# Edge counts beside the keys, x + b0 ahead of the degrees, and one more step inside layer 0's norm

## Chip, cores and metric

The kernel runs on one core of one Trainium2 chip, in one launch. The metric is the device time of that launch in microseconds; it was 4014.03 us before the change (median of 3 runs, 4009.7 to 4014.95).

## What is computed

Two graph layers over 32 batches of 512 nodes with 128 features; the adjacency has about one edge in sixteen and its diagonal. Cut to what matters:

```
# layer 0
a = adj + I;  degree = a.sum(2);  d = degree ** -0.5  (0 where infinite)
x = layernorm(x + d * (a @ (d * (x @ weight))) + bias)
# layer 1, for every pair of nodes i, j
pre = (x @ W1[:D])[j] + (x @ W1[D:])[i] + b1
msg = gelu(layernorm(pre) * g1 + be1)
agg[i] = sum over j of msg[i, j] * adj[i, j]
x = layernorm(x + layernorm(concat(x, agg) @ W2 + b2) * g2 + be2)
```

## The kernel before

**The sparse pairs.** Layer 1 does not form all pairs. For each node it picks the neighbours that exist, in 8 slots for each quarter of the nodes, one slot for the diagonal and two shared slots. The main loop runs over 32 batches, and in each over 41 *groups* (`order`: 8 slots of 4 groups, 1, and 2 of 4). Below, group k of a batch is the k-th of these 41, counted from 0. A group is a chain over four engines: TensorE builds `u` (16 bf16 matmuls, L724 and L725), VectorE adds and brings it to SBUF (`u_sb`, L734), ScalarE takes the gelu (`m`, four instructions at L763), GpSimd multiplies the selection with the adjacency (`sw`, L749), and TensorE adds it up (`agg`, L772). The chain is spread over the loop: iteration k issues u of group k, then `pass_on` issues agg of group k-3, u_sb and sw of group k-1 and m of group k-2. Three PSUM buffers hold u, so u of group k waits for u_sb of group k-3.

**The preparation.** While batch b runs its groups, batch b+1 is prepared by Python generators whose steps end at `yield`. `prepare(g)`, at the end of each iteration, advances them in the order of the list `plan`: layer0, lists, parts, factors, more, shared. A phase with n steps over w groups has done `n * (j + 1) // w` of them after its j-th group, so its step k (from 0) falls in group ceil(w(k+1)/n) - 1. `layer0` of batch b+1 has 26 steps over the groups 0 to 21 of batch b. `advance(todo)`, just before `prepare`, moves the generator `finish` of the batch that ended last.

**Steps of layer0, as far as they matter here.** Steps 1 to 4 transpose the adjacency on TensorE (`pa`, L249); one step later ScalarE sums rows (`copied`, L260) and copies the transpose (`a_t`, L261). Step 5 does this for the last quarter and lets VectorE make `mask` from the whole of `a_t` (L263). Step 6 is empty. Step 7 has the degrees on GpSimd (L277 to L287) and `xb` = x + b0 (L289), then on ScalarE four `counted` (L293, each sums one quarter of the mask into `edges`), `s` (L297) and `own_s` (L302). Steps 9 and 10 issue the two halves of `pconv` on TensorE (L311). Step 11 has `y` and its statistics on VectorE (L318, L194, L196); the norm's GpSimd part (L199 to L205) is step 12, its ScalarE part `x1` (L208) step 13; `x1` is transposed on TensorE (`pt_x1`, L220) in step 15. From step 21 on, each step makes a quarter of `key` on VectorE from a matmul `pv` (L361 to L365).

**Other work of the same groups.** `finish` of the batch before uses the same `layernorm` twice: `un` and, as the last, `o_sb`, with VectorE statistics, a GpSimd part and a ScalarE part, all at the same line numbers as layer 0's. `more` (L455 to L458) keeps VectorE at searching neighbours beyond the eighth, `shared` (L466 to L598) follows; in it ScalarE copies `sent` (L533) behind TensorE's `pl` (L537). The `edges` are read much later, in `shared` (L499).

**What sets the order.** Inside `manual_schedule` VectorE, ScalarE and GpSimd execute in the order of the program text. TensorE and the DMA queue of SyncE are ordered by the framework's scheduler. Every engine executes its own queue in order, and an instruction whose input is late holds back all behind it. Single-buffered tiles by tag (`t1`, `t2`, `t3`, `mask`, `copied`, `xs`) add waits for the last reader.

Of the kernel before, what the change touches and what calls it, by code (L numbers as in the profile page):

```python
# [8 lines left out]
F32 = mybir.dt.float32  # L9
BF16 = mybir.dt.bfloat16  # L10
I32 = mybir.dt.int32
U32 = mybir.dt.uint32
AF = mybir.ActivationFunctionType
ALU = mybir.AluOpType
# [4 lines left out]
P = 128  # L19
# [8 lines left out]
def bcast(ap, n):  # L28

    return ap.unsqueeze(1).to_broadcast([ap.shape[0], n, ap.shape[-1]])  # L30
# [16 lines left out]
def sparse_path(ctx, tc, x, adj, w0, b0, w1, b1, g1, be1, w2, b2, g2, be2, out, most):  # L47
# [21 lines left out]
    nc = tc.nc  # L69
    B, N, D = x.shape  # L70
    C = N // P
# [3 lines left out]
    node = ctx.enter_context(tc.tile_pool(name="node", bufs=1))  # L75
    small = ctx.enter_context(tc.tile_pool(name="small", bufs=2))
# [66 lines left out]
    rows = {}  # L143
# [41 lines left out]
    def rsqrt(dst, src):  # L185

        nc.gpsimd.tensor_tensor(dst, src, power[:, 0:1].to_broadcast([P, src.shape[-1]]), ALU.pow)  # L187

    def layernorm(src, dst, key):

        stats = small.tile([P, C, 6], F32, tag="stats", name=f"stats_{key}")
        mv = small.tile([P, C, 2], F32, tag="mv", name=f"mv_{key}")
        for c in range(C):
            nc.vector.bn_stats(stats[:, c, :], src[:, c, :])  # L194
        for c in range(C):
            nc.vector.bn_aggr(mv[:, c, :], stats[:, c, :])  # L196
        yield
        ve = small.tile([P, C], F32, tag="ve", name=f"ve_{key}")
        nc.gpsimd.tensor_scalar(ve, mv[:, :, 1], EPS, None, ALU.add)  # L199
        rstd = small.tile([P, C], F32, tag="rstd", name=f"rstd_{key}")  # L200
        rsqrt(rstd, ve)

        shift = small.tile([P, C], F32, tag="shift", name=f"shift_{key}")
        nc.gpsimd.tensor_tensor(shift, mv[:, :, 0], rstd, ALU.mult)  # L204
        nc.gpsimd.tensor_scalar(shift, shift, -1.0, None, ALU.mult)  # L205
        yield
        for c in range(C):
            nc.scalar.activation(  # L208
                dst[:, c, :], src[:, c, :], AF.Identity, bias=shift[:, c : c + 1], scale=rstd[:, c : c + 1]
            )  # L210
        yield

    def bank(key):
        return ps.tile([P, 512], F32, tag="ps", name=key)
# [6 lines left out]
        return pt  # L221

    state = {}

    def pause(n):

        for _ in range(n):
            yield

    def layer0(b):  # L230

        st = state[b] = {}
        xs = node.tile([P, C, D], F32, tag="xs", name=f"xs_{b}")
# [7 lines left out]
        edges = small.tile([P, C], F32, tag="edges", name=f"edges_{b}")  # L241
        st["edges"] = edges
        deg = small.tile([P, C], F32, tag="deg", name=f"deg_{b}")
        mask = big.tile([P, C, N], BF16, tag="mask", name=f"mask_{b}")
        px = transposed(xs, f"x_{b}")
        for mc in range(C):
# [12 lines left out]
            copied = small.tile([P, N], BF16, tag="copied", name=f"copied_{b}_{mc}", bufs=1)  # L259
# [11 lines left out]
            if mc == 0:  # L271
                x_t = node.tile([P, N], F32, tag="t0", name=f"x_t_{b}")
                nc.scalar.copy(x_t, px)
        yield from pause(2)

        deg1 = small.tile([P, C], F32, tag="deg1", name=f"deg1_{b}")
        nc.gpsimd.tensor_scalar(deg1, deg, 1.0, None, ALU.add)  # L277
# [7 lines left out]
        nc.gpsimd.tensor_sub(dinv, rdeg, none)  # L285
        dinv2 = small.tile([P, C], F32, tag="dinv2", name=f"dinv2_{b}", bufs=1)
        nc.gpsimd.tensor_tensor(dinv2, dinv, dinv, ALU.mult)  # L287
        xb = node.tile([P, C, D], F32, tag="t2", name=f"xb_{b}")
        nc.gpsimd.tensor_tensor(xb, xs, bcast(rows["b0"], C), ALU.add)  # L289

        for q in range(C):
            copied = small.tile([P, N], BF16, tag="copied", name=f"counted_{b}_{q}", bufs=1)
            nc.scalar.activation(copied, mask[:, q, :], AF.Copy, accum_out=edges[:, q : q + 1])  # L293

        s = node.tile([P, C, D], F32, tag="t1", name=f"s_{b}")
        for c in range(C):
# [4 lines left out]
        for c in range(C):  # L301
            nc.scalar.activation(  # L302
                own_s[:, c, :], psup[:, c * P : (c + 1) * P], AF.Copy, scale=dinv2[:, c : c + 1]
            )
        yield from pause(2)
        nc.gpsimd.tensor_tensor(xb, xb, own_s, ALU.add)
        pt = bank(f"pconv_{b}")
# [8 lines left out]
        y = node.tile([P, C, D], F32, tag="t3", name=f"y_{b}")  # L316
        for c in range(C):
            nc.vector.scalar_tensor_tensor(  # L318
                y[:, c, :], pt[:, c * P : (c + 1) * P], dinv[:, c : c + 1], xb[:, c, :], ALU.mult, ALU.add
            )  # L320
        x1 = node.tile([P, C, D], F32, tag="x1", name=f"x1_{b}", bufs=3)
        yield from layernorm(y, x1, f"l0_{b}")
        st["x1"] = x1
        yield
        pt = transposed(x1, f"x1_{b}")
# [31 lines left out]
        key = big.tile([P, C, N], F32, tag="key", name=f"key_{b}")  # L357
        for q in range(C + 1):
            if q:
                here = key[:, q - 1, :]  # L360
                nc.vector.scalar_tensor_tensor(here, pt, a_sum[:, q - 1 : q], c_sum, ALU.add, ALU.add)  # L361
                nc.vector.scalar_tensor_tensor(here, here, -TINY, mask[:, q - 1, :], ALU.min, ALU.mult)
            if q < C:
                pt = bank(f"pv_{b}_{q}")
                nc.tensor.matmul(pt, at2[:, q * P : (q + 1) * P], ct, start=True, stop=True)  # L365
            yield
# [94 lines left out]
    def shared(b):  # L461
# [27 lines left out]
        first = small.tile([P, C * C], F32, tag="first", name=f"first_{b}", bufs=1)  # L489
        nc.scalar.copy(first, pt[:, : C * C])  # L490
        yield from pause(2)
        last = small.tile([P, C * C], F32, tag="last", name=f"last_{b}", bufs=1)
        nc.vector.tensor_tensor(last, first, count, ALU.add)
# [136 lines left out]
    def finish(b):  # L630

        st = state.pop(b)
        aggt = st["aggt"]
        pt = bank(f"pu_{b}")
        for c in range(C):
            o, here = pt[:, c * P : (c + 1) * P], slice(c * P, (c + 1) * P)
            nc.tensor.matmul(o, st["x1t"][:, here], w2_sb[:, 0, :], start=True, stop=False)
            nc.tensor.matmul(o, aggt[:, here], w2_sb[:, 1, :], start=False, stop=True)
        yield
        u = node.tile([P, C, D], F32, tag="f0", name=f"u_{b}")  # L640
        nc.vector.tensor_tensor(u, pt.rearrange("p (c d) -> p c d", d=D), bcast(rows["b2"], C), ALU.add)
        yield
        un = node.tile([P, C, D], F32, tag="f1", name=f"un_{b}")
        yield from layernorm(u, un, f"l1_{b}")
        nc.gpsimd.tensor_tensor(un, un, bcast(rows["g2"], C), ALU.mult)
        yield
        nc.gpsimd.tensor_tensor(un, un, bcast(rows["be2"], C), ALU.add)
        yield
        nc.gpsimd.tensor_tensor(un, un, st["x1"], ALU.add)
        yield  # L650
        o_sb = node.tile([P, C, D], F32, tag="f0", name=f"o_sb_{b}")
        yield from layernorm(un, o_sb, f"l2_{b}")
        yield
        nc.sync.dma_start(out[b].rearrange("(c p) d -> p c d", p=P), o_sb)
# [129 lines left out]
    def advance(gens, steps=1):  # L784
# [12 lines left out]

    n_groups = len(order)
    plan = [
        (layer0, 26, -n_groups, -19),  # L800
        (lists, 21, -19, -8),
        (parts, 7, -19, -10),
        (factors, 7, -8, -3),
# [265 lines left out]
def kernel(  # L1069
# [32 lines left out]
    with ExitStack() as inner:  # L1102
        sparse_path(inner, tc, *args, most)
# [42 lines left out]
```

## Time and profile before

| | us |
|---|---|
| median of 3 runs | 4014.03 |
| the profiled execution | 4011.64 |
| its span, first to last instruction | 4009.9 |
| the four counts of a batch (L293), 128 in all | 80.1, and 23.8 for reading their sums |
| xb (L289), 32 in all | 40.7 |
| mask (L263), 32 in all | 39.0 |
| layer 0's ScalarE norm (L208 x), 128 in all | 52.7, idle before them 104.2 |

The profile is of one execution. In a timeline line the numbers are the start and the length in us, then engine, line, operation, output and inputs, shapes, and how many instructions were merged; brackets give the engine's idle time before them and what ended it. Names lose their batch numbers, so `x` at L208 and in pt_x is x1. Engines are PE (TensorE matmul), DVE (VectorE), ACT (ScalarE), POOL (GpSimd) and SP (SyncE). The ends of matmuls are modelled and overlap a little. A batch takes 122 to 124 us: the first gelu of one batch starts at 1294.56 us and that of the next at 1418.02 us.

### The profile page before, as it was taken

Reading aid. Unit: us, or ns where it says so; the run is one execution under the profiler, and the core shown is the slowest. Engines: PE = TensorE matmul, PEld = TensorE weight load, DVE = VectorE, ACT = ScalarE, POOL = GpSimd, SP = SyncE. Lnnn points to the kernel's source line nnn. Section 1 sums busy time; section 2 is a strip of 40 time slices with the busy share of each in tenths; the row PEclk is TensorE's granted clock in tenths of the full one; section 3 lists DMA queues with packets and bytes.
Section 4 is the critical chain, followed back from the end, with each engine's and each line's share of the span. In section 5 each row is a group of like instructions: output and inputs, shape, how many; then the busy total and the mean of one; then the engine's idle time right before and its main releaser. Section 6 shows DMA issues by size and latency. Waiting matters only on the chain. (4 is left out here: it accounts for less than half of the span.)

```text
span 4009.9 us, 108439 instructions
## 1 busy us (share of the span) xinstructions
PE 3766.3 (94%) x39744; PEld 3510.3 (88%) x39744; DVE 3263.9 (81%) x10645; ACT 2791.9 (70%) x8321; POOL 2225.5 (55%) x2526
## 2 busy tenths in 40 slices
PE   5999999999999999999999999999999999999997
PEld 5988889888899888898888998888998889888887
DVE  6888888888887888888888888888888888788892
ACT  4777677676776766776767767667767677676664
POOL 4555565555655555655556555556555565555554
PEclk7999999999999999999999999999999999999998
DMA  3444444444444444444444444444444444444442
GB/s 85 107 109 106 114 101 106 107 107 105 113 102 106 108 106 110 106 106 106 107 105 113 102 106 108 106 112 104 106 105 108 105 108 106 108 107 105 98 105 56
DMA packets 902107, 419.99 MB, mean 105 GB/s; under 512 B 724304, under 2 KB 882192, under 8 KB 901568
## 3 DMA queue, kind: packets, MB, share of 16 engines
q1 hardware_dynamic: 901344, 412.52, 44.1%
q8 instruction: 317, 5.19, 0.5%
q14 instruction: 222, 1.82, 0.1%
q0 software_dynamic: 224, 0.46, 0.1%
HBM read 227.15 MB, written 13.76 MB: 60 GB/s over the span
## 5 line engine op out<-in xcount | busy, mean ns | idle before, releaser
L749 POOL TENSOR_TENSOR sw<-mt,a_t 128x512 f32<-128x512 bf16 x1056 | 1216.8, 1164 | 918.1 <-PE agg L772 764.0
L772 PE MATMUL agg<-sw,m 128*128 128x128 f32 x10496 | 1495.7, 285 | 76.2 <-POOL sw L749 46.1
L724 PE MATMUL u<-c,s 128*128 128x128 bf16 x15744 | 1433.9, 220 | 84.0 <-DVE u_sb L734 80.3
L763 ACT ACTIVATE m<-u_sb,r 128x128 f32<-128x128 f32 x4096 | 1294.0, 395 | 142.3 <-DVE u_sb L734 57.8
L772 PEld LDWEIGHTS agg<-sw,m 128*128 128x128 f32 x10496 | 1304.5, 192 | 94.2 <-POOL sw L749 51.3
L724 PEld LDWEIGHTS <-s 128*128 128x128 bf16 x15744 | 1191.2, 98 | 115.0 <-issue 40.9
L725 PE MATMUL u<-be,sd_rows 128*128 128x128 bf16 x5248 | 1148.6, 220 | 20.7 <-DMA sd_rows<-sd_ds 14.6
L734 DVE TENSOR_TENSOR u_sb<-u,ac 128x512 f32<-128x512 f32 x1056 | 713.4, 676 | 200.6 <-PE u L725 177.1
L725 PEld LDWEIGHTS <-sd_rows 128*128 128x128 bf16 x5248 | 512.7, 98 | 30.7 <-issue 20.0
L763 ACT ACTIVATE m<-u,r_s 128x128 f32<-128x128 f32 x1024 | 288.3, 363 | 251.6 <-PE agg L772 247.4
L533 ACT COPY sent<-pl 128x352 f32<-128x352 f32 x512 | 228.9, 447 | 315.9 <-PE pl L537 278.8
L687 DVE TENSOR_SCALAR s<-raw,node_p 128x2052 bf16<-128x2052 bf16 (+1 forms) x352 | 421.5, 1197 | 20.6 <-DMA raw<-idx_ds 11.9
L720 PE MATMUL u<-ac,sj 128*128 128x128 f32 x2048 | 437.8, 296 | 0.0
L749 POOL TENSOR_TENSOR sw<-mt,sent 128x512 f32<-128x512 bf16 x256 | 296.4, 1163 | 229.0 <-PE agg L772 176.2
L537 PEld LDWEIGHTS pl<-a_t,sj 128*128 128x128 f32 x2048 | 316.2, 191 | 60.7 <-issue 59.2
L457 DVE MAX8 a_t<-key 128x8 f32<-128x128 f32 x1024 | 301.2, 294 | 34.5
L537 PE MATMUL pl<-a_t,sj 128*128 128x176 f32 x2048 | 327.4, 313 | 1.3 <-POOL a_t L505 1.3
L522 DVE TENSOR_SCALAR sj<-pj,node_p 128x512 f32<-128x512 f32 x256 | 187.7, 745 | 153.8 <-PE pj L526 153.8
L720 PEld LDWEIGHTS u<-ac,sj 128*128 128x128 f32 x2048 | 310.0, 192 | 0.4
L458 DVE FIND_INDEX8 idx_m<-a_t,key 128x8 uint32<-128x128 f32 x1024 | 291.4, 285 | 0.0
L311 PEld LDWEIGHTS pconv<-s,a_t 128*128 128x128 f32 x1024 | 141.3, 214 | 57.1 <-ACT s L297 55.4
L361 DVE SCALAR_TENSOR_TENSOR key<-pv,a_sum,c_sum 128x512 f32<-128x512 f32 x128 | 95.7, 748 | 108.3 <-PE pv L365 108.3
(178 smaller groups left out, 4788.8 us busy)
## 6 DMA issues: line engine op xcount, KB each, us to landing
raw<-idx_d SPq DMA_DIRECT2D x256, 513.0 KB
raw<-idx_ds SPq DMA_DIRECT2D x64, 513.0 KB
a_nat<-in_adj_dram SPq DMA_DIRECT2D x32, 1024.0 KB
sd_rows<-sd_d SPq DMA_DIRECT2D x768, 12.0 KB
xs<-in_x_dram SPq DMA_DIRECT2D x32, 256.0 KB
out_dram<-o_sb SPq DMA_DIRECT2D x32, 256.0 KB
mt<-s SPq DMA_TRANSPOSE x352
raw<-idx_ds SPq DMA_DIRECT2D x32, 129.0 KB
```

The lines of the kernel that those rows point to most:

```text
L457: nc.vector.max(found, k)
L458: nc.vector.max_index(idx[:, n, h : h + 8], found, k)
L533: nc.scalar.copy(sent[:, n - 1], pt[:, : SHARED * WIDE].rearrange("p (k w) -> p k w", w=WIDE))
L537: nc.tensor.matmul(pt[:, k * WIDE : (k + 1) * WIDE], sj[:, n, k * P : (k + 1) * P], at[:, n, :], start=True, stop=True,)
L687: nc.vector.tensor_scalar(s.rearrange("p (k e) -> p k e", k=3), raw, node_p, None, ALU.is_equal)
L720: nc.tensor.matmul(pu[:, c, :], place, state[b]["ac"][:, q, 0, :], start=first, stop=False)
L724: nc.tensor.matmul(pu[:, c, :], here, c3[:, k, c, :], start=(first and k == 0), stop=False)
L725: nc.tensor.matmul(pu[:, c, :], dev[:, q, c, :], be9, start=False, stop=(c == C - 1))
L734: nc.vector.tensor_tensor(u, pu, a if t == EXTRA else bcast(a[:, q, :], C), ALU.add)
L749: nc.gpsimd.tensor_tensor(sw, mt[:, 0] if t == EXTRA else mt[:, :, q, :], a, ALU.mult)
L763: nc.scalar.activation(m[:, c, :], u[:, c, :], AF.Gelu, scale=r[:, k : k + 1])
L772: nc.tensor.matmul(st["agg"][:, c, :], m[:, c, :], sw[:, c, :], start=(begin and c == 0), stop=(end and c == C - 1),)
```

## The change

Four edits. The counts of edges leave step 7 of `layer0` and go, one by one, in front of the four quarters of `key`. `xb` goes into a step of its own ahead of the degrees, in the place of one of the two empty yields. `layernorm` takes a number of yields between its GpSimd and its ScalarE part, and layer 0 passes 2 instead of 1. And the plan gives `layer0` 27 steps, over the same 22 groups.

```diff
-    def layernorm(src, dst, key):
+    def layernorm(src, dst, key, waits=1):
...
         nc.gpsimd.tensor_scalar(shift, shift, -1.0, None, ALU.mult)
-        yield
+        yield from pause(waits)
         for c in range(C):
             nc.scalar.activation(
...
-        yield from pause(2)
+        yield
+        xb = node.tile([P, C, D], F32, tag="t2", name=f"xb_{b}")
+        nc.gpsimd.tensor_tensor(xb, xs, bcast(rows["b0"], C), ALU.add)
+        yield
 
         deg1 = small.tile([P, C], F32, tag="deg1", name=f"deg1_{b}")
...
         nc.gpsimd.tensor_tensor(dinv2, dinv, dinv, ALU.mult)
-        xb = node.tile([P, C, D], F32, tag="t2", name=f"xb_{b}")
-        nc.gpsimd.tensor_tensor(xb, xs, bcast(rows["b0"], C), ALU.add)
-
-        for q in range(C):
-            copied = small.tile([P, N], BF16, tag="copied", name=f"counted_{b}_{q}", bufs=1)
-            nc.scalar.activation(copied, mask[:, q, :], AF.Copy, accum_out=edges[:, q : q + 1])
...
-        yield from layernorm(y, x1, f"l0_{b}")
+        yield from layernorm(y, x1, f"l0_{b}", 2)
...
             if q:
+
+                copied = small.tile([P, N], BF16, tag="copied", name=f"counted_{b}_{q}", bufs=1)
+                nc.scalar.activation(copied, mask[:, q - 1, :], AF.Copy, accum_out=edges[:, q - 1 : q])
                 here = key[:, q - 1, :]
...
-        (layer0, 26, -n_groups, -19),
+        (layer0, 27, -n_groups, -19),
```

`pause(n)`, which yields n times, moves up unchanged so that `layernorm` can call it.

More of the change, by code (lines that the diff above doesn't have):

```diff
@@ L187, in rsqrt, with pause @@
         nc.gpsimd.tensor_tensor(dst, src, power[:, 0:1].to_broadcast([P, src.shape[-1]]), ALU.pow)
-    def layernorm(src, dst, key):
+    def pause(n):
+        for _ in range(n):
+            yield
+    def layernorm(src, dst, key, waits=1):
         stats = small.tile([P, C, 6], F32, tag="stats", name=f"stats_{key}")
@@ L223, in sparse_path @@
     state = {}
-    def pause(n):
-        for _ in range(n):
-            yield
     def layer0(b):
@@ L273, in layer0 @@
                 nc.scalar.copy(x_t, px)
-        yield from pause(2)
+        yield
+        xb = node.tile([P, C, D], F32, tag="t2", name=f"xb_{b}")
+        nc.gpsimd.tensor_tensor(xb, xs, bcast(rows["b0"], C), ALU.add)
+        yield
         deg1 = small.tile([P, C], F32, tag="deg1", name=f"deg1_{b}")
```

## Prediction

> **What bounds the kernel now.** I read the page's first lines, then the waits of PE, then one batch (first gelu at 1294.56 us) engine by engine in the timeline, then the granted clock.
>
> ```profile
> PE 3766.3 (94%) x39744; PEld 3510.3 (88%) x39744; DVE 3263.9 (81%) x10645; ACT 2791.9 (70%) x8321; POOL 2225.5 (55%) x2526
> ```
> ```profile
> PE u L724 <- DVE u_sb L734: 80.3, 69, 2.2
> PE agg L772 <- POOL sw L749: 46.1, 30, 1.6
> PE agg L772 <- ACT m L763: 30.0, 20, 1.5
> ```
>
> PE is the bound: it idles 4009.9 - 3766.3 = 244 us. These three rows are 156 of it, and each occurs in every batch, in the same three places. In the batch that I followed:
>
> ```profile
> 1308.35 0.33 PE L724 MATMUL u<-c,s 128*128 128x128 bf16 x3 [0.84 <-DVE u_sb L734]
> 1310.90 0.22 PE L724 MATMUL u<-c,s 128*128 128x128 bf16 x1 [1.50 <-DVE u_sb L734]
> 1325.70 1.27 PE L772 MATMUL agg<-sw,m 128*128 128x128 f32 x8 [1.52 <-ACT m L763]
> 1326.82 0.60 PE L220 MATMUL pt_x<-ident,x 128*128 128x128 f32 x4
> 1330.06 1.16 PE L772 MATMUL agg<-sw,m 128*128 128x128 f32 x8 [1.54 <-POOL sw L749]
> ```
>
> PE loses 0.84 + 1.50 + 1.52 + 1.54 = 5.4 us here, between 1307 and 1330, and hardly anything in the rest of the batch: from 1331 to 1363 it is busy for 31.99 of 32.00 us. So what the change is worth is the start of the agg of group 11 (1330.06): what moves it moves the batch. The engines behind those waits:
>
> ```profile
> 1300.52 0.36 DVE L196 BATCH_NORM_AGGREGATE mv_l<-stats_l 128x2 f32<-128x6 f32 x4
> 1304.52 1.22 DVE L263 TENSOR_SCALAR mask<-a_t 128x2048 bf16<-128x2048 f32 x1
> 1317.07 0.67 DVE L734 TENSOR_TENSOR u_sb<-u,ac 128x512 f32<-128x512 f32 x1
> 1321.19 0.35 DVE L196 BATCH_NORM_AGGREGATE mv_l<-stats_l 128x2 f32<-128x6 f32 x4
> ```
> ```profile
> 1321.63 0.23 POOL L199 TENSOR_SCALAR ve_l<-mv_l 128x4 f32<-128x4 f32 x1 [3.34 <-DVE mv_l L196]
> 1324.81 0.23 POOL L199 TENSOR_SCALAR ve_l<-mv_l 128x4 f32<-128x4 f32 x1
> ```
> ```profile
> 1303.60 0.57 ACT L261 COPY a_t<-pa 128x512 f32<-128x512 f32 x1
> 1323.62 1.65 ACT L208 ACTIVATE x<-y,shift_l,rstd_l 128x128 f32<-128x128 f32 x4 [3.27 <-POOL shift_l L205]
> 1326.79 1.65 ACT L208 ACTIVATE o_sb<-un,shift_l,rstd_l 128x128 f32<-128x128 f32 x4 [0.35 <-POOL shift_l L205]
> ```
>
> DVE is full: from 1297 to 1330 it never waits. It makes u_sb late (the first two PE waits) and the norm's mv_l late (1321.54); POOL's in-order ve_l waits 3.34 us for it and holds sw back (the last PE wait), and ACT's x1 waits 3.27 us for the shift and holds m back (the third).
>
> **The change, part by part.** *The plan first,* since it moves things that the diff does not name. With 27 steps, step k is in group ceil(22(k+1)/27) - 1. The step of the last a_t quarter and mask goes from group 5 to 4, where its ACT copies now stand ahead of m of group 3 and its mask directly behind the mv_l that ends at 1300.88; the second half of pconv goes from 9 to 8, y from 10 to 9; GpSimd's norm stays in 10; x1 goes from 11 to 12, there behind o_sb; pt_x1 stays in 13. The built program has its instructions in this order, on all engines and in every batch.
>
> *Counts.* On ACT four counts take 2.87 us (1307.37 to the start of s at 1310.24) and leave a stretch where ACT is not what PE waits for. Each lands ahead of a sent copy, where ACT idles 1.93 us until PE's pl; one count needs 0.72 us. Price 0; without that cover 31 x 4 x 0.72 = 89 us.
>
> *x + b0.* 1.27 us of POOL, now ahead of sw of group 5: that sw starts at 1304.12 instead of 1302.89, the degrees end at 1308.7 instead of 1307.5. ACT reaches s at about 1310.7, so nothing waits; uncovered, 1.2 us a batch. SP's load of xs waits for xb; it is now ahead of the transpose in SP's queue, released at 1304.2, while the transpose can't go before 1307.4. Price 0.
>
> *The mask.* In group 4 ACT runs m of group 2, copied and a_t of the third quarter, then at 1301.81 copied of the fourth and at 1302.42 its a_t, done at 1302.98. DVE is free for the mask at 1300.88 and starts it at 1303.03: a new wait of 2.15 us, on the engine that has no slack. Behind it stand two steps of more, the one-hot of L687 and u_sb of group 4. Before, DVE needed 1317.07 - 1300.80 = 16.27 us from the end of mv_l to u_sb of group 8, the mask included and without a gap; so that u_sb now starts at 1303.03 + 16.27 = 1319.30, 2.23 us later. PE: u of group 7 needs u_sb of group 4, which ends at 1307.95 instead of 1304.60, a PE wait of 2.3 us in place of the first two; further waits of 0.7 (u of group 8) and 0.65 (u of group 12) follow.
>
> *The norm.* y and its statistics stand one u_sb and the statistics of o_sb earlier in DVE's order: 1319.30 + 0.59 + 1.01 + 0.78 + 0.35 = 1322.03 for mv_l, against 1321.54. POOL, whose order here is unchanged: ve_l at 1322.12, its chain 1.92, sw of group 10 at 1324.04, ve_l for o_sb at 1325.30 (1.26 later, as before), shift done at 1327.25. ACT no longer waits for x1 ahead of m of group 10, which runs 1324.4 to 1325.7. But o_sb waits for its shift until 1327.27, x1 follows 1.55 later at 1328.82 and ends at 1330.47. PE has done agg of group 10 by 1326.5 and stands at pt_x1 until x1 comes: a new wait of 2.8 us, then four transposes at ACT's pace. Behind pt_x1 in PE's queue are pj (starts 1330.61), u of group 14 and agg of group 11: 1330.61 + 0.22 + 0.89 = 1331.72 against 1330.06. That is **+1.66 us a batch**, 31 batches: +51.5 us. After it all engines are paced by PE, so nothing gives it back.
>
> *The clock.* PE's granted clock falls in windows of 3.41 us; here is one batch where it did:
>
> ```profile
> 2043.56:2046.97 3.41, 1.28 (x19) 1.16 (x19) 3.25 (x14) 3.31 (x12) 3.41 (x4) 1.00 0.77 239
> 2046.97:2050.39 3.42, 3.42 (x18) 3.29 (x18) 3.33 (x7) 3.42 (x13) 3.42 (x3) 0.50 0.01 5
> 2050.39:2053.80 3.41, 3.41 (x36) 3.35 (x36) 3.38 (x7) 1.83 (x8) 3.41 (x4) 1.00 0.00 0
> ```
>
> (PE busy comes first after the length; the clock is third from the end.) A window with PE busy 1.28 us is followed by one at 0.50, where 18 matmuls run instead of 36. After the first 100 us of the trace every window with PE busy for 1.5 us or less was followed so, and none above 1.7. Before, this hit a stretch where PE had slack. The new wait has 2.8 us plus 0.4 between transposes; wherever the window's edge falls, one side holds over 1.8 us of idle in some 9 of 10 batches, and the slow window lies on work where PE is the bound. It costs half of the slow time: 1.3 to 1.7 us where the slow window starts behind the gap, 0.5 to 1.3 where part of it falls inside. I take 1.0 us a batch, +31 us; ends 0 and 1.5 (0 and 47 us).
>
> The Trainium skill (TensorE: Matmul & The Clock Gate, section "Why this matters for your kernels") asks only that PE gaps stay under about 3 us. By it the 2.8 us wait would cost no clock, and the sum would be the first rival's below; the rows above (1.28 us busy, and no single gap over 1.5 us) go against it, and I follow them.
>
> *Start.* In the first batch s waits behind the counts (19.54); dinv is there at 18.35: -1.2 us, once.
>
> Sum: 4011.64 (span 4009.9 and 1.7 around it) + 51.5 + 31 - 1.2 = 4093. The median of the runs is 2.4 us above the profiled execution: **4095 us**.
>
> **Rivals.** *The clock stays* (0.27): dips fall where PE waits anyway, as before. 4014 + 51.5 - 1.2 = 4064. *The further step does its work* (0.09), faster: a single mechanism, x1 ready when PE arrives at pt_x1 (1326.8). Then the waits of 1.52 and 1.54 both go, 31 x 3.06 = 95 us, 3919. It decides from the moment that o_sb's shift is there by 1323.6, 3.6 us earlier than I have it; were only the mask's wait absent, POOL's chain would end at 1325.0 and agg of group 11 start at 1329.5, 17 us in all, 3997. For it speaks that ACT's 3.27 us are plainly there to be had; against it that DVE has no gap in which the 2.15 us could vanish. *The counts bind* (0.04): if they hold back the sent copies until PSUM banks run out, 89 us more, 4184; the 1.93 us of idle speak against it. *The losses cancel* (0.04): the DVE wait is half as long and the clock holds, within 0.2% of 4014.
>
> **How the numbers follow.** My forecast has 0.56. Its own range: 1.66 +/- 0.3 and 0.6 to 1.5 us a batch give 4074 to 4120. The range 4052 to 4118 takes in the first rival and leaves out the others. 0.2%, about 8 us, is what a measurement of this kernel can tell. Slower: 0.56 + 0.27 + 0.04 = 0.87; same 0.04; faster 0.09.
>
> **What would show it.** Right: DVE mask waits about 2.1 us for a_t; PE waits for u_sb some 2.3 us at u of group 7 and for x1 at pt_x1 some 2.8; the waits of agg for sw and m are gone; the clock drops in most batches near 1331 of this one. Wrong: mask without a wait, or pt_x1 without one; then the kernel is not slower. ACT waiting less for pl and PE for a PSUM bank at pl would show the counts.

## The result and the profile after

| | before | after |
|---|---|---|
| median of the runs side by side, us | 4011.86 (4 runs, 4008.56 to 4014.95) | 4145.79 (4 runs, 4144.2 to 4148.21) |
| ratio, 95% interval | | 1.0332 [1.032, 1.0345] |
| span of the profiled execution, us | 4009.9 | 4145.1 |
| start of one batch to the next, mean of 30 (from the second batch on), us | 122.63 | 127.05 |

The change makes the kernel 134 us slower. The prediction had the sign and the chain right (4095), but the time lies above its range (4052 to 4118).

The first lines of the page after:

```profile
span 4145.1 us, 108407 instructions
PE 3847.1 (93%) x39744; PEld 3570.4 (86%) x39744; DVE 3330.1 (80%) x10645; ACT 2786.7 (67%) x8321; POOL 2231.0 (54%) x2526
```

PE executes the same 39744 matmuls, yet is busy for 80.8 us more, and DVE for 66 us more with as many instructions as before. Something made single instructions longer: on DVE the mask (39.0 to 68.6 us in all) and `last` (L494, 128x16; 5.1 to 29.4 us). The waits of PE (line and tile that waited, engine, tile and line waited for; us in total, times, longest):

```profile
PE u L725 <- DVE u_sb L735: 126.3, 69, 3.4
PE pt_x L226 <- ACT x L214: 84.1, 31, 4.9
```

The waits of agg for sw and m are gone from the head of the list, as predicted, and pt_x1 waits in their place. Now the followed batch in the timeline. Its first gelu starts at 1336.72 instead of 1294.56; "+" below is the time from there, so +8.49 is 1345.21.

```profile
1345.06 1.28 POOL L277 TENSOR_TENSOR xb<-xs,b_row 128x512 f32<-128x512 f32 x1
1345.21 2.21 DVE L264 TENSOR_SCALAR mask<-a_t 128x2048 bf16<-128x2048 f32 x1 [2.15 <-ACT a_t L262]
1346.29 2.16 POOL L750 TENSOR_TENSOR sw<-mt,a_t 128x512 f32<-128x512 bf16 x1
...
1351.22 0.33 PE L725 MATMUL u<-c,s 128*128 128x128 bf16 x3 [3.38 <-DVE u_sb L735]
...
1362.62 0.67 DVE L735 TENSOR_TENSOR u_sb<-u,ac 128x512 f32<-128x512 f32 x1
...
1370.65 1.65 ACT L214 ACTIVATE o_sb<-un,shift_l,rstd_l 128x128 f32<-128x128 f32 x4 [1.61 <-POOL shift_l L211]
1372.21 1.63 ACT L214 ACTIVATE x<-y,shift_l,rstd_l 128x128 f32<-128x128 f32 x4
1372.74 1.63 PE L226 MATMUL pt_x<-ident,x 128*128 128x128 f32 x4 [2.81 <-ACT x L214]
1374.59 0.53 PE L725 MATMUL u<-c,s 128*128 128x128 bf16 x3
1376.29 2.02 PE L773 MATMUL agg<-sw,m 128*128 128x128 f32 x8
```

The mask waits 2.15 us for a_t and starts at +8.49; the prediction said 2.15 and 1303.03 (+8.47). But it then takes 2.21 us, and before it took 1.22. GpSimd had started xb 0.15 us ahead of it, and the sw behind xb takes 2.16 us where it took 1.17. The ends stand one behind the other: xb to 1346.34, 1.08 us more to the mask's end at 1347.42, 1.03 us more to sw's at 1348.45, as if one engine stood while the other worked. In the profile such standing is no idle time: it is counted into the instruction. From here everything on DVE's path is about 1.2 us later than predicted, 1.0 of it the mask: u_sb of group 8 at +25.90 (predicted +24.74), x1 done at +37.12 (+35.91), pt_x1's last transpose behind it.

The last three lines have the second surprise: three matmuls of u take 0.53 us instead of the 0.33 of earlier in the batch, the eight of agg 2.02 instead of 1.11. The windows of the granted clock (length, busy time of PE, PEld, DVE, ACT, POOL, then the clock):

```profile
1368.95:1372.37 3.42, 0.98 (x9) 0.79 (x8) 3.42 (x13) 1.81 (x6) 2.98 (x8) 1.00 0.07 25
1372.37:1375.78 3.41, 3.04 (x17) 2.10 (x18) 3.41 (x8) 3.41 (x11) 3.41 (x4) 0.50 0.25 48
1375.78:1379.19 3.41, 3.41 (x20) 2.80 (x19) 1.22 (x3) 2.05 (x7) 2.20 (x3) 0.50 1.04 239
```

A window with PE busy for 0.98 us is followed by two at half speed. Summed over the trace, without the first 100 us and the last 20, PE was granted half speed for 238 us in all 31 batches, and before for 58 us in 12 of them. Of the 238 us, 123 lie beside pt_x1, in each of the 31 batches, and 109 at +13 to +16, behind the wait for u_sb, in 25 of them.

Agg of group 11 starts at +39.57 instead of +35.51: 4.06 us late, and the prediction had 1.66. The rest of the batch adds 0.36 to that on average.

### The profile page after: what moved, and what is told of

It reads as the page before. It is cut to its first block, busy times and chain, and to the rows that moved or that the text cites. A ratio compares the mean times of both kernels' runs of the same rounds, so it can differ in the third digit from the quotient of the medians.

```text
span 4145.1 us, 108407 instructions
## 1 busy us (share of the span) xinstructions
PE 3847.1 (93%) x39744; PEld 3570.4 (86%) x39744; DVE 3330.1 (80%) x10645; ACT 2786.7 (67%) x8321; POOL 2231.0 (54%) x2526
## 5 line engine op out<-in xcount | busy, mean ns | idle before, releaser
L750 POOL TENSOR_TENSOR sw<-mt,a_t 128x512 f32<-128x512 bf16 x1056 | 1254.4, 1197 | 994.2 <-PE agg L773 763.1
L725 PE MATMUL u<-c,s 128*128 128x128 bf16 x15744 | 1452.8, 224 | 130.9 <-DVE u_sb L735 126.3
L773 PE MATMUL agg<-sw,m 128*128 128x128 f32 x10496 | 1511.6, 287 | 0.0
L725 PEld LDWEIGHTS <-s 128*128 128x128 bf16 x15744 | 1222.0, 101 | 221.1 <-issue 151.2
L773 PEld LDWEIGHTS agg<-sw,m 128*128 128x128 f32 x10496 | 1324.1, 196 | 7.3
L726 PE MATMUL u<-be,sd_rows 128*128 128x128 bf16 x5248 | 1169.0, 224 | 21.3 <-DMA sd_rows<-sd_ds 15.0
L726 PEld LDWEIGHTS <-sd_rows 128*128 128x128 bf16 x5248 | 525.6, 100 | 31.5 <-issue 20.0
L401 DVE FIND_INDEX8 idx<-top,key 128x8 uint32<-128x128 f32 x512 | 145.6, 285 | 0.0
```

Source lines behind the costliest of these rows:

```text
L725: nc.tensor.matmul(pu[:, c, :], here, c3[:, k, c, :], start=(first and k == 0), stop=False)
L726: nc.tensor.matmul(pu[:, c, :], dev[:, q, c, :], be9, start=False, stop=(c == C - 1))
L750: nc.gpsimd.tensor_tensor(sw, mt[:, 0] if t == EXTRA else mt[:, :, q, :], a, ALU.mult)
L773: nc.tensor.matmul(st["agg"][:, c, :], m[:, c, :], sw[:, c, :], start=(begin and c == 0), stop=(end and c == C - 1),)
```

## The experiments

Ratios are to the kernel before, with 95% intervals; it ran beside every experiment, with medians from 4009.94 to 4013.94 us, so a difference between two of the kernels is good to about 4 us. "Half speed" is the sum described above.

### Where the mask is late, and what it meets

**xb back in its old place,** the rest of the change kept:

```diff
-        xb = node.tile([P, C, D], F32, tag="t2", name=f"xb_{b}")
-        nc.gpsimd.tensor_tensor(xb, xs, bcast(rows["b0"], C), ALU.add)
         yield
...
         nc.gpsimd.tensor_tensor(dinv2, dinv, dinv, ALU.mult)
+        xb = node.tile([P, C, D], F32, tag="t2", name=f"xb_{b}")
+        nc.gpsimd.tensor_tensor(xb, xs, bcast(rows["b0"], C), ALU.add)
```

> The changed kernel with x + b0 back behind dinv2. Theory (mask on VectorE can't run while any GpSimd instruction of about 1 us over SBUF runs): in its new place mask starts 0.14 us after sw of group 5 instead of 0.15 us after xb, so it still takes about 2.2 us in place of 1.22, and the time stays at 4130 to 4150 us. Rival (it is xb alone that slows mask): mask takes 1.22 us, VectorE gains 1.0 us a batch, 31 us in all, 4105 to 4120 us.

Measured 4135.24 us, 1.0311 [1.0295, 1.0326]. The mask still takes 2.04 us on average: sw of group 5 now stands where xb stood. So it is not xb as such: sw does it too, and behind sw GpSimd's `deg` (128x4) now takes 1.20 us where it took 0.23. Taking xb away gives only 10.6 us.

**The mask one step later:**

```diff
-            if mc == C - 1:
-                nc.vector.tensor_scalar(mask...)
...
         yield
+        nc.vector.tensor_scalar(mask...)
         xb = node.tile([P, C, D], F32, tag="t2", name=f"xb_{b}")
```

> The changed kernel with mask issued one step later, so in group 5 as before. Theory (the early mask sets u_sb, the norm and with them x1): no wait of mask for a_t (2.15 us before); mask now meets sw of group 5 on GpSimd and takes about 1.95 us; agg of group 11 starts 0.2 us later than in the kernel before, and PE still stands about 2.8 us at pt_x1 and loses some 1.4 us to the clock: 4045 to 4070 us. Rival 1 (the early mask is all of it): 4012 us or less. Rival 2 (the mask's place does not matter, x1 behind o_sb is all of it): above 4110 us.

Measured 4039.13, 1.0073 [1.0057, 1.0088]. The wait for a_t is gone, the mask takes 1.82 us on average, and agg of group 11 starts between +35.1 and +36.3 although PE waits at pt_x1 as long as after (84.6 us). The mask one step too early is worth 107 us of the 134, the wait behind it and all that follows counted.

**GpSimd made to stand while the mask is made.** This one adds an instruction to the changed kernel and takes nothing away:

```diff
         yield
+        held = small.tile([P, C], F32, tag="held", name=f"held_{b}", bufs=1)
+        nc.gpsimd.tensor_scalar(held, mask[:, C - 1, N - C :], 1.0, None, ALU.add)
         xb = node.tile([P, C, D], F32, tag="t2", name=f"xb_{b}")
```

> The whole change with one GpSimd instruction added ahead of xb: it adds 1 to the last four columns of the mask, into a tile that nobody reads, so that GpSimd stands still until VectorE has finished the mask; xb and the sw behind it then run after the mask and not beside it. Nothing is taken away, and GpSimd loses about 1.4 us a batch. Theory (mask and xb exclude each other, which made the mask 1.0 us longer): the mask still starts at +8.5 behind its wait of 2.15 us for a_t, but takes 1.22 us instead of 2.20; u_sb of group 8 comes at about +24.9 instead of +25.9, agg of group 11 at about +38.5 instead of +39.57; 1.0 to 1.5 us a batch, time 4100 to 4120. Rival (the mask is long in this place for another reason, as that it reads what ACT has just written): mask at 2.2 us, time 4140 or more. A third possibility: the mask is short, but the later xb and sw lengthen the small instructions behind it by as much; then u_sb of group 8 stays within 0.3 us of +25.9, and the time within 10 us of 4146.

Measured 4114.11, 1.0255 [1.0238, 1.0272], 31.7 us less than the changed kernel. Its timeline:

```profile
1335.90 1.23 DVE L264 TENSOR_SCALAR mask<-a_t 128x2048 bf16<-128x2048 f32 x1 [2.15 <-ACT a_t L262]
...
1337.40 1.27 POOL L279 TENSOR_TENSOR xb<-xs,b_row 128x512 f32<-128x512 f32 x1
1338.63 1.16 POOL L752 TENSOR_TENSOR sw<-mt,a_t 128x512 f32<-128x512 bf16 x1
```

Same place, same wait of 2.15 us, but the mask takes 1.23 us and sw 1.16. From the first start to the last end, mask, xb and sw took 3.39 us side by side in the changed kernel (1345.06 to 1348.45); their own times here add up to 3.66. So at most 0.27 us of them overlapped. u_sb of group 8 comes at +24.92, agg of group 11 starts at +38.54. That mask and GpSimd's work exclude each other is shown, and here it costs 1.0 us a batch. Half speed falls as well, from 238 to 136 us: mostly at +13 to +16, before PE comes to stand at pt_x1 anyway, but also from 123 to 96 us beside pt_x1, so a few of the 31.7 us may be the clock's. `last` stays long here (0.93 us on average); what it costs no run shows.

### What the wait at pt_x1 costs

**x1 ahead of the further step,** so that it stands in front of o_sb again:

```diff
-        yield from layernorm(y, x1, f"l0_{b}", 2)
+        yield from layernorm(y, x1, f"l0_{b}")
         st["x1"] = x1
         yield
+        yield
```

> The changed kernel with its further step behind x1 instead of in front of it: x1 in group 11 ahead of m of group 10, all else where it is. Theory (x1 behind o_sb costs the wait at pt_x1 and the clock after it): PE's wait at pt_x1 goes from 2.7 us to nothing, agg of group 11 then waits for sw some 2 us; it starts 1.7 us later than in the kernel before, plus about 0.4 us of clock: 4060 to 4085 us. Rival (the VectorE delay alone sets the end): 4130 us or more.

Measured 4064.23, 1.0133 [1.0118, 1.0149]. Agg of group 11 starts at +37.23; half speed falls to 154 us. The waits of PE:

```profile
PE u L726 <- DVE u_sb L736: 121.2, 62, 3.4
PE agg L774 <- POOL sw L751: 47.2, 30, 1.6
```

The early waits for u_sb stay, pt_x1's is gone, agg's for sw is back. x1 behind o_sb costs 82 us here.

**The changed kernel with PE kept busy at pt_x1:**

```diff
-        pt = transposed(x1, f"x1_{b}")
+        pt = bank(f"pt_x1_{b}")
+        for _ in range(36):
+            nc.tensor.matmul(pt[:, :P], ident_h, ones_h, start=True, stop=True)
+        for c in range(C):
+            nc.tensor.transpose(pt[:, c * P : (c + 1) * P], x1[:, c, :], ident)
```

> The whole change with 36 matmuls of 128x128 on constants added into pt_x1's bank, directly ahead of its four transposes and behind the agg of group 10, where PE waits 2.8 us in every batch of the changed kernel. They add about 36 x 0.06 = 2.2 us of PE work to a place where PE has nothing to do, and take nothing else away. Theory (the wait at pt_x1 costs through the clock too: the window after it runs at half speed): the window near +36 to +38 is granted full speed, the transposes take 0.25 us instead of 1.63 and u of group 9 0.9 instead of 1.9; about 1.5 us a batch, 45 us in all, time 4090 to 4115. Rival (the half-speed windows only fill time in which PE would wait for other things): time within 0.3% of the changed kernel, 4133 to 4158. If the added matmuls cost more than the clock gives: over 4158.

Measured 4100.35, 1.0224 [1.0207, 1.0241]: 1152 more matmuls, and 45.4 us less. In the timeline (its batch starts at 1324.83):

```profile
1357.87 2.17 PE L325 MATMUL pt_x<-ones_h,ident_h 128*128 128x128 bf16 x36
1360.84 1.48 PE L327 MATMUL pt_x<-ident,x 128*128 128x128 f32 x4 [0.80 <-ACT x L214]
...
1362.38 0.33 PE L729 MATMUL u<-c,s 128*128 128x128 bf16 x3
```

x1 and so pt_x1 come no earlier, but u takes 0.33 us again and agg of group 11 starts at +38.44. The transposes did not shrink to 0.25 us as I had written: they follow ACT's quarters of x1, at any clock. Half speed falls from 238 to 119 us: none is left beside pt_x1, and what is left lies in most batches at +13 to +16, behind the wait for u_sb. That the clock is a cost of its own is shown: 1.46 us a batch for the half speed beside pt_x1. What the other half costs no run shows.

**The whole change, only the mask late,** a dozen groups later beside the squares:

```diff
-            if mc == C - 1:
-                nc.vector.tensor_scalar(mask...)
...
         yield
+        nc.vector.tensor_scalar(mask...)
         asq = node.tile([P, N], F32, tag="t1", name=f"asq_{b}")
```

> The whole change with one thing altered: DVE's mask instruction stands beside the squares in group 16, a dozen groups later, where nothing waits for it soon; x1 keeps its place behind o_sb and the further step stays ahead of it. Theory (the early mask is the larger part of the loss, because it waits 2.15 us for a_t and then shares its time with GpSimd): u_sb of group 8 returns to about +21.6 as with the mask late and 26 steps, shift and o_sb follow, x1 ends near +32.8 and the agg of group 11 starts near +34.0, 1.5 us ahead of before; the remaining loss to the version with x1 first is that PE still waits at pt_x1. Time 3970 to 4010, ratio 0.99 to 1.00. Rival (x1 behind o_sb loses by itself, whatever the mask does): the wait at pt_x1 stays at 2.5 us or more a batch, half-speed windows stay near 35, time 4012 or more.

Measured 4006.91, 0.9989 [0.9979, 0.9998]. It lies inside the range of the theory, and what marks the rival is there too, so the two were no alternatives. The mask takes 1.22 us, u_sb of group 8 is at +21.58 and x1 ends at +32.80 as expected, but:

```profile
PE pt_x L226 <- ACT x L214: 84.3, 31, 4.9
PE agg L772 <- POOL un L645: 36.7, 30, 1.2
```

PE waits at pt_x1 as long as ever, since it arrives earlier by what x1 gained. Agg of group 11 starts at +34.99 where I had +34.0; I had not counted the half speed behind that wait (109 us).

### The three parts alone

**x + b0 ahead, alone,** on the kernel before:

> The kernel before with x + b0 alone moved ahead of the degrees. Theory (mask and GpSimd exclude each other): sw of group 5 now runs when mask wants to start, mask takes 1.9 to 2.0 us, VectorE is 0.75 us later up to the norm, 31 x 0.75 = 23 us: 4030 to 4040 us. Rival (moving xb is free, as predicted): mask 1.22 us, 4012 us within 0.2%.

Measured 4024.63, 1.0035 [1.0021, 1.0049], under what I expected. The mask meets sw here too and takes 1.82 us on average (xb is over 0.35 us before it starts), but in the batch that I followed u_sb of group 8 moves by only 0.05: other DVE instructions (over at 0.78 us instead of 1.31) gain most of it back; probably because xb's second half no longer falls beside them, which I did not follow.

**The counts beside the keys, alone:**

> The kernel before with the counts alone moved beside the keys. Theory (they leave a place where ScalarE has slack and go to one where it waits for pl): 4012 us within 0.3%. Rival (ahead of the sent copies they hold back PE's PSUM banks): up to 89 us more, 4100 us, with waits of PE at pl for sent.

Measured 4020.73, 1.0023 [1.0013, 1.0034], a small loss where I expected none. The waits of PE:

```profile
PE agg L771 <- ACT m L762: 76.0, 31, 2.5
PE u L723 <- DVE u_sb L733: 51.2, 69, 2.2
```

ACT's cover at pl did its part (sent waited 278.8 us before, 221.6 here). But PE now loses in one piece at agg what it had lost in two, 2.49 us in the followed batch, and half speed rises from 58 to 106 us.

**The further step with the 27 steps, alone:**

```diff
-        yield
+        yield from pause(waits)
...
-        yield from layernorm(y, x1, f"l0_{b}")
+        yield from layernorm(y, x1, f"l0_{b}", 2)
...
-        (layer0, 26, -n_groups, -19),
+        (layer0, 27, -n_groups, -19),
```

> The kernel before with the 27 steps and the longer pause in layer 0's norm, counts and x + b0 left alone. Theory (the plan's shift is what costs): mask waits 2.15 us for a_t and takes about 2.2 us beside sw of group 5, PE waits at pt_x1: as slow as the whole change or slower, 4130 to 4200 us, since s now also stands behind the counts. Rival (counts or x + b0 carry the loss): below 4080 us.

Measured 4083.52, 1.0178 [1.0162, 1.0193]. This is a miss: it lies below the theory's range, 62 us under the whole change. The mask is as long (2.04 us) and waits as much (66.5 us), but three other DVE lines are much cheaper. The groups of this kernel (us in total, mean ns of one, idle before them), and then of the kernel after:

```profile
L469 DVE SCALAR_TENSOR_TENSOR over<-a_t,sharing 128x256 f32<-128x256 f32 x32 | 15.3, 477 | 0.0
L474 DVE TENSOR_SCALAR here<-top 128x128 f32<-128x128 f32 x32 | 8.1, 253 | 0.0
L479 DVE TENSOR_SCALAR counts<-a_t 128x4 f32<-128x4 f32 x32 | 6.5, 202 | 0.0
```
```profile
L470 DVE SCALAR_TENSOR_TENSOR over<-a_t,sharing 128x256 f32<-128x256 f32 x32 | 46.1, 1442 | 0.0
L480 DVE TENSOR_SCALAR counts<-a_t 128x4 f32<-128x4 f32 x32 | 28.9, 904 | 0.0
L475 DVE TENSOR_SCALAR here<-top 128x128 f32<-128x128 f32 x32 | 23.2, 725 | 0.0
```

Together 2.1 us less a batch for the same work. With the counts still on ACT, un and own_s come later, GpSimd waits for them (1.32 us for own_s in the followed batch), and is idle just when DVE makes these three. In the whole change GpSimd has something to do there, and DVE's 128x4 instruction takes 0.9 us instead of 0.2. But of the 2.1 us only 0.66 reach x1 (its end is at +36.45 in the median batch, +37.11 in the whole change): y now waits for pconv, 43.9 us in 22 batches. The rest of the gain looks like the clock. PE's wait at pt_x1 is 49.5 us instead of 84.1 in all, and half speed beside pt_x1 falls from 123 to 17 us. With 0.66 x 31 = 20 us for x1, and the 45 us that filling the wait gave above, the 62 us are there. No run separates the two, but they can explain why the parts alone add up to only 72.5 + 14.7 + 9.7 = 97 of 134 us.

### Can the step be had without its loss

**The mask late and the counts beside the keys, 26 steps, xb and the norm as before:**

> The kernel before with the counts beside the keys and mask moved from the transposes to the step of the squares (group 16), 26 steps, x + b0 and the pause as before. Theory (VectorE is what sets agg of group 11): 1.13 us less on VectorE ahead of it, agg of group 11 1.1 us earlier, 35 us in all: 3970 to 3985 us. Rival (GpSimd or ScalarE hold it for reasons of their own): within 0.3% of 4012 us.

Measured 3978.9, 0.9924 [0.9909, 0.9939]. The mask takes 1.22 us again, u_sb of group 8 comes at +21.6 instead of +22.51 and agg of group 11 starts at +34.62.

**The same with 27 steps, the further step behind x1:**

```diff
         st["x1"] = x1
         yield
+        yield
...
-        (layer0, 26, -n_groups, -19),
+        (layer0, 27, -n_groups, -19),
```

> As e7_mask_late, with 27 steps and the further step behind x1: x1 stays in group 11 ahead of m of group 10, y and its statistics come one group earlier, pt_x1 stays. Theory: mv_l is ready when GpSimd reaches ve_l, x1 no longer waits, and agg of group 11 waits for sw alone, until about 2.9 us earlier than in the kernel before: 3900 to 3960 us. Rival (an earlier y takes from PE what it gives, since all of pconv then stands ahead of u of group 9): no faster than e7_mask_late.

Measured 3929.58, 0.98 [0.9785, 0.9815]: 216 us under the change, close to the sum of the mask's place (4145.79 - 4006.91 = 139) and of x1's (82). Half speed is down to 14 us, the batch at 119.91 us. The waits of PE that are left:

```profile
PE agg L771 <- ACT m L762: 47.7, 60, 1.0
PE agg L771 <- POOL sw L748: 46.8, 30, 1.6
```

**And missed, most and place later,** so that sw of group 11 is not behind them:

```diff
-        nc.gpsimd.tensor_tensor(missed, missed, st["edges"], ALU.add)
...
-        nc.gpsimd.tensor_tensor(place, place, over, ALU.mult)
...
+        nc.gpsimd.tensor_tensor(missed, missed, st["edges"], ALU.add)
...
+        nc.gpsimd.tensor_tensor(place, place, over, ALU.mult)
         sj_f = sj.rearrange("p n e -> p (n e)")
```

> The version that was fastest so far (change with the mask in the step of the squares and x1 ahead of the further step) with one more edit: GpSimd's missed, most and place, seven instructions of the keys' chain, are issued in the step ahead of sj instead of with over, here and counts, so that the sw of group 11 is no longer behind them. Theory (in that version agg of group 11 waits 1.56 us for sw, and nothing else is late there): the wait goes or falls under 0.4 us, the batch is 1.2 to 1.6 us shorter, 37 to 50 us in all, time 3880 to 3900, ratio 0.967 to 0.973. Rival (u or y is late next, or the chain of keys then comes too late for sj): time 3915 or more.

Measured 3914.52, 0.9761 [0.9744, 0.9777], the fastest of all, yet a miss: 15 us instead of 30 to 50. The wait for sw is gone and agg of group 11 starts 1.20 us earlier, at +31.68, but a batch is only 0.42 us shorter. Small waits follow that were not there (0.37 us for m at the same agg, 0.32 at pj, some at pidx). They do not make up all of the 0.8; the rest I did not trace.

## Why the prediction was wrong in size

| step of the prediction | predicted | measured |
|---|---|---|
| mask waits for a_t | 2.15 us | 66.4 / 31 = 2.14 |
| mask's own time | 1.22, as before | 2.14 on average |
| u_sb of group 8, after its place before | +2.23 | +3.39; with GpSimd held, +2.41 |
| PE at u of group 7 | 2.3 | 3.38; with GpSimd held, 2.40 |
| PE at pt_x1 | 2.8 | 2.81 |
| start of agg of group 11 | +1.66 | +4.06 |
| clock, a batch | 1.0, ends 0 and 1.5 | 1.46 |
| first gelu of the kernel | -1.2 | +2.4; of the second batch +3.3, where each later batch loses 4.42 |

**Right:** the plan's shifts, the wait for a_t and its length, ACT's order of o_sb and x1, the new wait at pt_x1 (its 2.81 us by luck in part: x1 and PE's arrival there were both some 1.2 us later than predicted), that agg no longer waits for sw and m, and that nothing behind gives the loss back. The rival with the x1 that is ready in time comes near in another kernel, the one with the mask late and x1 first (3929.58 against its 3919), but that is luck: the two waits of agg that were to go are still there (47.7 and 46.8 us), and what went are the waits for u_sb, from 80.3 to 8.6 us, and half speed, from 58 to 14 us.

**The step that failed** is the one that carried the mask's 1.22 us of before (it is inside the 16.27 us) to its new place, and priced *x + b0* ahead of sw at 0. I asked whether anybody waits for these instructions, and never what runs beside them. DVE's mask and GpSimd's xb and sw exclude each other, so putting one beside the other made the mask 2.14 us on average and added 1.0 us to the engine that I had called full. By the run with GpSimd held this is 31.7 us. The mask's new place is the larger part of it: with xb back in its old place the mask met sw and took 2.04 us, and only 10.6 us came back.

**Mis-sized:** the clock, 1.0 us a batch against 1.46, 45.4 us where I had 31. I had a slow window beside pt_x1 in 9 of 10 batches, and it came in all 31. The rule that no window above 1.7 us of PE work was followed by half speed holds in the trace before only for windows at full speed: of those already at half speed, two with PE busy for 2.92 and 2.14 us (from 2903.72 and 3910.65) were followed by another. **Wrong and small:** the start. In the first batch of the changed kernel the four counts still stand ahead of s (16.69 to 19.67; s starts at 19.58, before at 19.54), so the 1.2 us were not there to be had. The counts at price 0 are not quite that either: alone they cost 9.7 us, with joined waits and more half speed.

The sum with these terms: 51.5 (predicted) + 31.7 + 45.4 = 129 of 134 us. With GpSimd held u_sb of group 8 still comes 0.18 us a batch later than predicted (+2.41 against +2.23), which would be 5 or 6 us more. The two runs were each made on the changed kernel by itself, so how their terms overlap is not shown.

The Trainium skill has the rule that I passed over: SBUF — State Buffer, section "Who interferes with whom", says that VectorE and GpSimd share one pair of SBUF ports as an exclusive lock for a whole instruction. By that page a VectorE instruction takes part if it has two SBUF inputs (against GpSimd instructions that read SBUF) or runs in a two-port mode, which a tensor_scalar can enter. The traces agree with the lock in these rows: mask 1.22 or 2.2 us, over 0.42 or 1.47, here 0.22 or 0.74, and on the other side sw 1.17 or 2.16 us. It does not hold for every pair: the tensor_scalar `s` (128x2052, bf16 to bf16) ran beside GpSimd work for 0.2 us or more in 223 of its 320 instances before and never took more than 1.28 us. Which port is held is not shown by any run here, only the exclusion.

The other page that the prediction weighed (TensorE: Matmul & The Clock Gate, section "Why this matters for your kernels") would have let a 2.81 us gap pass. Here the wait at pt_x1 was followed by half speed in all 31 batches, and filling it gave 45 us.

## What to carry to other kernels

When an instruction is moved, look at what runs beside it on the other of VectorE and GpSimd, not only at who waits for it: the same instruction may take twice its time there, and the profile books it as busy. A line whose shortest instance is far under its mean is the sign, and it stood in the trace before: over took 1.32 to 1.43 us in 31 batches and 0.43 in one. The mask itself showed it there, from the other side:

```profile
1304.65 1.15 POOL L281 TENSOR_TENSOR degp<-deg,none 128x4 f32<-128x4 f32 x1
```

The mask had started 0.13 us before it and ended at 1305.74, 0.06 us before it did; in the changed kernel, away from the mask, the same 128x4 instruction takes 0.20 us in the median.

An edit that turns two short waits of TensorE into one long one can be worth less than their sum says, because the clock falls behind the long one (the counts alone took half speed from 58 to 106 us); where the wait cannot go, matmuls on constants in it can pay.

## What I had not expected of the hardware

- VectorE and GpSimd side by side: an instruction of 128x4 elements took 0.16 us where it started with GpSimd idle and 0.93 us beside it; 128x2048 to bf16 took 1.22 and 2.21 us.
- Adding a wait made the kernel faster: GpSimd held for 1.42 us in the followed batch, 31.7 us saved in all.
- Adding 2.17 us of matmuls a batch made it faster by 1.46 us a batch.
